# Two sparse-graph hops on one core: sources multiplied ahead of a branch, rows fetched earlier, own links added later

## The chip, the cores and the metric

The kernel runs on one core of one Trainium2 chip. The metric is the device time of one execution in microseconds; smaller is better. The engines are named as in the profile: PE (TensorE, with its weight loads as PEld), DVE (VectorE), ACT (ScalarE), POOL (GpSimd) and SP (SyncE, which here issues most of the DMAs). Each runs its own list of instructions in order, and they meet through semaphores.

## The reference, cut to what matters

Layer 0 is a graph attention over 4096 nodes, layer 1 a two-step diffusion. The part that the change touches is the second: in each step the features `Xf` are multiplied by the normalised 0/1 matrix `R` (the adjacency plus the unit matrix), and `Xa` by an attention matrix that keeps the top 90% of its probability.

```python
    R = S + jnp.eye(N, dtype=X.dtype)
    R = R / R.sum(-1, keepdims=True)
    Z = jnp.zeros_like(X)
    Xf = X
    Xa = X
    for n in range(STEPS):                     # STEPS = 2
        A = _top_p_attention(Xa, W1, W2, W3)
        Xf = R @ Xf
        Xa = A @ Xa
        Z = Z + Xf @ U1[n].T + Xa @ U2[n].T
    h = X + Z
    ...                                        # layer norm of h, and the sum with x
```

`X` is 4096 x 256 in float32, `S` the 4096 x 4096 adjacency.

## The kernel before, in words

Nodes are cut into NB = 32 blocks of 128 rows. Layer 0 comes first and leaves the adjacency in `adj_d`, arranged as 4 passes (`PASSES`) x 32 source blocks: the block `adj_d[p, :, j, :]` is 128 sources by 1024 targets, 512 KB. Then, for each step `n` of layer 1, there are two stages.

**A hop** (`R @ Xf`, lines 450 to 539). For each of the 128 pairs `(p, j)` in `order`, one edge block `ar` (every fifth one in a spare buffer, `aru`) and one row block of the source are needed. In hop 1 (step 0) the rows lie in SBUF as `X`. In hop 2 (step 1) they are read from `xf_d`, 128 KB each, into tiles named `x1` (three buffers) or `xa` (two). `fetched` (line 450) issues the two loads on SP, the edge block first. `split` (465) adds the unit matrix to the block where source and target coincide (line 468, on DVE; the "own link"), and cuts the source row into a high part (line 470, a cast on ACT) and the rest (line 471, on DVE), both in `hl`. `graph_products` (474) then multiplies: for each feature half `s` and term `t`, two matmuls, one for each 512 columns `c` of targets. The half `c = 0` is summed in the PSUM tile named `mm`, of which there are two with two banks each; the half `c = 1` in two tiles named `acc`. So there are 8 matmuls a source. `hops` (513) walks over the sources: in turn `n` it fetches source `n`, splits source `n - 1` and multiplies source `n - 5` (`LOOK = 4`); there are four `ar` buffers, one `aru`, and five of `hl`. It yields twice a source, and at each yield other work is put between the products: projections to keys and queries (`projections`, 592), tables of moments (lines 646 to 695, among them the copy of `mu` on line 660), the logits and exponentials of the first three attention blocks (`fills`, 1109; lines 578 and 738) and their search for a threshold (`picks`, 1129; lines 800, 824 and 831). At the end of a pass `drained` (480) copies the sums out.

**The attention** of the 32 blocks (lines 1209 to 1230). `attend` (941) transposes the exponentials in 8 groups (`turn`, line 911 on PE, copied to `eT` on ACT), multiplies them with `X` (`gather`, line 919), and runs the functions that the dictionary `between` has for a group. `contributed` (936) and `finish` (1081) apply the weights and add up.

In this code the order on each engine is written out by hand: within `tc.manual_schedule` an engine issues its instructions in the order in which the Python text makes them.

**The branch.** Between the steps stands `repaired` (1074): if any row's threshold was not found, some blocks are computed again, with `prepared` (1021) and `completed` (1050). In the run shown nothing is computed again; every engine jumps over that code (line 1075). Past the jump each engine waits until its own earlier work is done and then raises its semaphores by what the code jumped over would have raised them. What comes after the branch and uses a tile that this code uses too (an `mm` or `acc` tile in PSUM, an `xa` tile) waits for those raised semaphores of the other engines. A first jump of the same kind, line 1206, lies in the last attention block of a step.

In before, hop 2's first three sources are fetched just ahead of the last contributions of step 0 (line 1226, `early`). Their splits stand ahead of line 1075 on ACT and DVE, their products behind it on PE.

Of the kernel before, what the change touches and what calls it, by code (L numbers as in the profile page):

```python
# [26 lines left out]
P = 128  # L27
# [13 lines left out]
G0 = 8  # L41
# [15 lines left out]
def gat_then_top_p_diffusion(  # L57
# [108 lines left out]
    with tc.tile_pool(name="l0", bufs=1) as l0, tc.tile_pool(name="l0s", bufs=2) as l0s, tc.tile_pool(name="l0o", bufs=1) as l0o:  # L166
# [280 lines left out]
        PASSES = NB // G0  # L447
        S = SimpleNamespace(spare=None)

        def fetched(hop, n, p, j):  # L450

            r = SimpleNamespace(j=j, p=p)
            if S.spare is not None and n % 5 == 4:
                r.ar = S.spare.tile([P, G0 * P], F32R, name="aru", tag="u")
            else:
                r.ar = rp.tile([P, G0 * P], F32R, name="ar", bufs=4)
            nc.sync.dma_start(r.ar.bitcast(F32), adj_d[p, :, j, :].bitcast(F32))
            if hop == 0:
                r.src = X[:, j, :]
            else:  # L460
                r.src = S.rows.tile([P, D], F32, name="x1", bufs=3) if n % 5 < 3 else S.rows.tile([P, D], F32, name="xa")
                nc.sync.dma_start(r.src, xf_d[j])
            return r

        def split(r):
            if r.j // G0 == r.p:
                own = r.ar[:, ts(r.j % G0, P)]
                nc.vector.tensor_tensor(own, own.bitcast(F32), ident, ALU.add)
            hl = rp.tile([P, 2, D], F32R, name="hl", bufs=5)
            nc.scalar.copy(hl[:, 0, :], r.src)  # L470
            nc.vector.tensor_tensor(hl[:, 1, :], r.src, hl[:, 0, :].bitcast(F32), ALU.subtract)
            return r.ar, hl

        def graph_products(j, s, acc, ar, hl):
            for t in range(2):
                for c in range(2):
                    nc.tensor.matmul(acc[c][s], hl[:, t, ts(s, P)], ar[:, ts(c, 512)],  # L477
                                     start=(j == 0 and t == 0), stop=(j == NB - 1 and t == 1))

        def drained(hop, p, acc):  # L480
# [30 lines left out]
        order = [(p, j) for p in range(PASSES) for j in range(NB)]  # L511

        def hops(hop, early=()):

            fetch, ready, turned = dict(enumerate(early)), {}, []
            parted = 0
            for n in range(len(order) + LOOK + 1):
                if len(early) <= n < len(order):
                    fetch[n] = fetched(hop, n, *order[n])
                m = n - LOOK - 1  # L520
                held = m // NB * NB + NB + 2 if m >= 0 and m % NB > NB - 4 else len(order)
                while parted < min(n, len(order), held):
                    ready[parted] = split(fetch.pop(parted))
                    parted += 1
                if m >= 0:
                    p, j = order[m]
                    if j == 0:
                        wide = ps2.tile([P, 2, 512], F32, name="mm")
                        acc = [[wide[:, s, :] for s in range(KC)],
                               [ps1.tile([P, 2, D], F32, name="acc").rearrange("p t d -> p (t d)") for s in range(KC)]]  # L530
                    graph_products(j, 0, acc, *ready[m])
                    if turned and j > 2 and j % 2:
                        turned.pop(0)()
                    yield
                    graph_products(j, 1, acc, *ready.pop(m))
                    if j == NB - 1:
                        turned = drained(hop, p, acc)
                    yield
            S.turned = turned

        first_hop = hops(0)
# [46 lines left out]
    def waits(n):  # L588
        for i in range(n):
            yield  # L590

    def projections(cur, n, G):
# [59 lines left out]
        for g in range(NB // 8):  # L652
            pg = ps2.tile([P, 2, 512], F32, name="mm")
            for i in range(8):
                nc.tensor.matmul(pg[:, i // 4, ts(i % 4, DA + 1)], qT[:, ts(8 * g + i, P)].bitcast(F32), moments, start=True, stop=True)
# [4 lines left out]
            nc.scalar.copy(mu[:, ts(g, 8)].rearrange("p (h i) -> p h i", h=2), of[:, :, :, 0])  # L660
# [31 lines left out]
        nc.vector.tensor_scalar(far, far, -1.0, 1.0, ALU.mult, ALU.add)  # L692
        nc.vector.tensor_scalar(sg, sg, 1.0 / 0.64, None, ALU.mult)
        G.kT, G.qT, G.sg = kT, qT, sg
        yield from waits(6)

    def table(name):
        return small.tile([P, NB], F32, name=name, bufs=1)
# [322 lines left out]
    def prepared(R):  # L1021

        act, dve = index(R, ET.Activation), index(R, ET.DVE)
        q = rows.tile([2 * DA, P], F32R, name="a_q", tag="q_s", bufs=3)
        shift = col("a_nm", 1)
        nc.scalar.copy(q, R.qT[:, ds(act * P, P)].bitcast(F32))
        q = (q, swapped(q))
        nc.scalar.copy(shift, R.nm[:, ds(act, 1)])
        nc.vector.tensor_copy(R.t, R.table[:, ds(dve, 1)])
        sums = small.tile([P, 2, 4], F32, name="sums", bufs=6)  # L1030
        ev = R.e.rearrange("p (h c n) -> p h c n", h=2, c=4)

        def exponentials_again():
            for c in range(4):
                nc.scalar.activation(ev[:, :, c, :], logits(q, R.kT, c), AF.Exp, bias=shift, accum_out=sums[:, c // 2, c % 2:c % 2 + 1])
            nc.vector.tensor_tensor(sums[:, 0, :2], sums[:, 0, :2], sums[:, 1, :2], ALU.add)
            nc.vector.tensor_tensor(R.z, sums[:, 0, 0:1], sums[:, 0, 1:2], ALU.add)

        exponentials_again()
        with tc.If(number(R, R.failed) > 0):  # L1040

            m = small.tile([P, N // 1024], F32, name="m4", bufs=1)
            for c in range(N // 1024):
                nc.vector.tensor_reduce(m[:, c:c + 1], logits(q, R.kT, c), AX.XY, ALU.max)
# [105 lines left out]
    for n in range(STEPS):  # L1150
# [2 lines left out]
        found = [table(f"found{i}") for i in range(3)]  # L1153
        blocks = {}
        with tc.manual_schedule(engines=every):
            pieces = first_hop if n == 0 else hops(n, early)
            filling, picking = fills(n, G, found, blocks), picks(n, found, blocks)
            done = 0 if n else NB - G0 - LOOK
            for i, _ in enumerate(pieces, 2 * done):
# [104 lines left out]
```

## Time and profile before

| what | us |
|---|---|
| median of 3 runs | 2985.69 (2983.98 to 2989.06) |
| the profiled execution | 2990.15 |
| its span, first to last instruction | 2988.2 |
| PE busy / PEld busy | 2844.6 / 2477.4 |
| DVE busy / ACT busy / POOL busy | 2199.6 / 1918.9 / 725.7 |
| hop 1, first to last start of its products | 839.6 to 1152.3 |
| hop 2, first to last start of its products | 1905.2 to 2238.0 |
| median landing of an edge block `ar` / a row from `xf_d` into `x1` | 4.7 / 4.9 |

The page gives each engine's busy time, then the span in 40 equal slices with a digit for the busy tenths of each, the DMA queues, the chain of work that ended last, and groups of instructions with the idle time before them and what ended most of it ("<-"). Other views of the same trace list the instructions in order of time, all instructions of one source line, who waited for whom, and the busy time in chosen stretches. A line such as `PE mm L615 <- ACT xs L610: 2.6, 4, 1.4` says that PE, before line 615, waited for ACT's line 610 for 2.6 us in total, 4 times, the longest 1.4 us. "PEldq", "DVEq" and so on are an engine's sequencer: waiting, branching or issuing.

### The profile page before, as it was taken

Reading aid. Unit: us, or ns where it says so; the run is one execution under the profiler, and the core shown is the slowest. Engines: PE = TensorE matmul, PEld = TensorE weight load, DVE = VectorE, ACT = ScalarE, POOL = GpSimd, SP = SyncE. Lnnn points to the kernel's source line nnn. Section 1 sums busy time; section 2 is a strip of 40 time slices with the busy share of each in tenths; the row PEclk is TensorE's granted clock in tenths of the full one; section 3 lists DMA queues with packets and bytes.
Section 4 is the critical chain, followed back from the end, with each engine's and each line's share of the span. In section 5 each row is a group of like instructions: output and inputs, shape, how many; then the busy total and the mean of one; then the engine's idle time right before and its main releaser. Section 6 shows DMA issues by size and latency. Waiting matters only on the chain. (4 is left out here: it accounts for less than half of the span.)

```text
span 2988.2 us, 51984 instructions
## 1 busy us (share of the span) xinstructions
PE 2844.6 (95%) x19033; PEld 2477.4 (83%) x19033; DVE 2199.6 (74%) x5187; ACT 1918.9 (64%) x3075; POOL 725.7 (24%) x1637
## 2 busy tenths in 40 slices
PE   4699999999999999999999999798899999999998
PEld 3499999999977778888888888676678888888887
DVE  6666877868754383888888889242755999999996
ACT  5767687867823735777777775234427777777772
POOL 3201101111010210233222331000203444444442
PEclk7799999999999999999999999999999999999999
DMA  6859668695455784000000000577991001000000
GB/s 153 176 208 238 193 217 190 232 226 189 179 169 163 245 298 144 19 26 19 19 19 19 26 19 19 172 240 218 307 320 30 25 27 30 25 25 25 31 25 21
DMA packets 181151, 368.15 MB, mean 123 GB/s; under 512 B 17168, under 2 KB 133904, under 8 KB 176784
## 3 DMA queue, kind: packets, MB, share of 16 engines
q1 hardware_dynamic: 129824, 261.55, 26.8%
q0 software_dynamic: 21504, 83.89, 11.8%
q10 hardware_dynamic: 29552, 19.22, 2.1%
q8 instruction: 155, 2.54, 0.4%
q14 instruction: 116, 0.95, 0.1%
HBM read 301.35 MB, written 109.38 MB: 137 GB/s over the span
## 5 line engine op out<-in xcount | busy, mean ns | idle before, releaser
L919 PE MATMUL acc<-X,eT 128*128 128x256 f32 x4096 | 965.8, 381 | 0.0
L919 PEld LDWEIGHTS acc<-X,eT 128*128 128x128 f32 x4096 | 743.2, 190 | 97.4 <-ACT eT L913 14.6
L325 PE MATMUL acc<-ut,m 128*128 128x195 bf16 (+1 forms) x8192 | 701.2, 247 | 13.6 <-DVE m L305 8.0
L325 PEld LDWEIGHTS <-m 128*128 128x128 fp8e4 x8192 | 696.9, 97 | 17.9 <-issue 9.6
L738 ACT ACTIVATE e<-mm,nm 128x1024 f32<-128x1024 f32 x256 | 286.9, 1121 | 301.8 <-PE mm L578 288.4
L299 ACT ACTIVATE g<-sr,d_big 128x1024 uint8<-128x1024 f32 x448 | 471.3, 1140 | 5.4 <-DMA s_d<-sT 2.9
L477 PE MATMUL mm<-ar,hl 128*128 128x512 f32 x844 | 342.8, 406 | 25.7 <-DVEq L1075 10.9
L806 DVE SCALAR_TENSOR_TENSOR big<-e,c 128x4096 f32<-128x4096 f32 x58 | 273.0, 4708 | 121.3 <-POOL c L791 84.1
L913 ACT COPY eT<-tp 128x512 f32<-128x512 f32 x512 | 299.3, 585 | 95.6 <-PE tp L911 94.6
L824 DVE MAX8 cand<-big 128x8 f32<-128x228 f32 (+1 forms) x1152 | 348.3, 380 | 0.0
L762 POOL TENSOR_TENSOR sums<-sums 128x2 f32<-128x2 f32 x64 | 12.7, 198 | 1343.3 <-ACT void L745 1343.3
L477 PE MATMUL acc<-ar,hl 128*128 128x512 f32 x844 | 334.2, 396 | 0.6 <-ACT stage L488 0.6
L911 PE MATMUL tp<-ident,e 128*128 128x128 f32 x2048 | 310.6, 274 | 2.7 <-PEq L1206 0.6
L911 PEld LDWEIGHTS tp<-ident,e 128*128 128x128 f32 x2048 | 248.6, 141 | 71.8 <-ACT eT L933 27.8
L305 DVE TENSOR_TENSOR m<-g,ax 128x512 uint32<-128x512 uint32 x256 | 181.5, 709 | 127.3 <-PE acc L325 104.0
L848 DVE SCALAR_TENSOR_TENSOR e<-e,found 128x4096 f32<-128x4096 f32 x58 | 259.6, 4477 | 0.0
L745 ACT ACTIVATE void<-e,c1x 128x2048 int8<-128x2048 f32 x128 | 257.4, 2011 | 3.3 <-issue 2.9
L745 ACT ACTIVATE void<-e,c 128x2048 int8<-128x2048 f32 x128 | 257.4, 2011 | 2.0 <-issue 2.0
L477 PEld LDWEIGHTS mm<-ar,hl 128*128 128x128 f32 x844 | 161.5, 191 | 68.4 <-issue 13.5
L578 PE MATMUL mm<-kT,qT 128*128 128x512 f32 x512 | 199.2, 470 | 11.4 <-ACT e L738 10.4
L306 DVE TENSOR_TENSOR m<-m,ax 128x512 uint32<-128x512 uint32 x256 | 177.1, 692 | 25.3
L477 PEld LDWEIGHTS acc<-ar,hl 128*128 128x128 f32 x844 | 161.6, 191 | 32.7 <-ACT stage L488 1.0
(262 smaller groups left out, 3457.6 us busy)
## 6 DMA issues: line engine op xcount, KB each, us to landing
ar<-adj_d SPq DMA_DIRECT2D x211, 512.0 KB, 4.7
adj_d<-ax POOLq DMA_DIRECT2D x32, 2048.0 KB, 7.0
ut<-uv_d SPq DMA_DIRECT2D x60, 784.0 KB, 5.4
aru<-adj_d SPq DMA_DIRECT2D x45, 512.0 KB, 4.8
ax<-in_adj_t_dram POOLq DMA_DIRECT2D x32, 512.0 KB, 15.8
x<-xf_d SPq DMA_DIRECT2D x78, 128.0 KB, 4.9
uv_d<-st ACTq DMA_DIRECT2D x32, 294.0 KB, 4.2
xf<-xft_d SPq DMA_DIRECT2D x64, 128.0 KB, 2.3
```

The source lines that it names most:

```text
L299: nc.scalar.activation(g[:, c, :], shared[k].sr, AF.Relu, scale=BIG, bias=d_big[:, h, j:j + 1])
L325: nc.tensor.matmul(shared[k].acc[i][:, t, :cols], m[t][:, c, ts(i, P)], shared[k].ut[j // QUARTER][:, j % QUARTER, t, :cols], start=(j == ...
L477: nc.tensor.matmul(acc[c][s], hl[:, t, ts(s, P)], ar[:, ts(c, 512)], start=(j == 0 and t == 0), stop=(j == NB - 1 and t == 1))
L578: nc.tensor.matmul(pm[:, h, :], q[t], kT[:, ds(h * (N // 2) + c * 512, 512)], start=(t == 0), stop=(t == 1))
L738: nc.scalar.activation(ev[:, :, c, :], r.pm[c], AF.Exp, bias=r.nm, accum_out=r.sums[:, c // 2, c % 2:c % 2 + 1])
L745: nc.scalar.activation(void, r.e[:, ts(h, N // 2)], (AF.Relu, AF.Sign)[i], bias=r.c1, scale=-1.0, accum_out=r.sums[:, h, 2 + i:3 + i])
L806: nc.vector.scalar_tensor_tensor(big, r.e, r.c3, r.e, ALU.is_le, ALU.mult, accum_out=r.low3)
L824: nc.vector.max(cand[:, s, :], big[:, edges[s]:edges[s + 1]])
L848: nc.vector.scalar_tensor_tensor(r.e, r.e, r.t, r.e, ALU.is_ge, ALU.mult, accum_out=kept)
L911: nc.tensor.transpose(pt[:, i, :], r.e[:, ts(4 * g + i, P)], ident)
L913: nc.scalar.copy(eT, pt)
L919: nc.tensor.matmul(r.acc[:, 0, :], eT[:, i, :], cur[:, j, :], start=(j == 0), stop=(j == NB - 1))
```

## The change

- `fetched` becomes two functions, `source` (the row) and `edge` (the block). In turn `n` the row of source `n + 2` is fetched, and then the edge block of source `n`.
- `split` only cuts rows. The own link is added by `own`, which in turn `n` goes up to source `n - 3`; its product comes two turns later.
- `begin(second, 4)`, put at group 2 of the last attention block of step 0, issues the rows and edges of hop 2's first four sources. Their splits follow at groups 5 and 6, their own links at group 6.
- After that block's `contributed`, PE multiplies these four sources with the half `c = 0` of the targets: 16 matmuls, before the branch. After the branch the first four sources have only the half `c = 1` left (16 matmuls). The `mm` tile of the first half is held across the branch.
- In `prepared`, which lies inside the branch, products go through single PSUM banks named `tp` instead of `mm`: 8 pieces of 512 columns in place of 4 of 1024.
- The copy of `mu` moves from ACT to DVE, and the tables are followed by 10 yields instead of 6.

```diff
+        def source(A, n):
+            if n in A.src or n >= len(order):
+                return
+            if A.hop == 0:
+                A.src[n] = X[:, order[n][1], :]
+            else:
+                A.src[n] = S.rows.tile([P, D], F32, name="x1", bufs=3) if n % 5 < 3 else S.rows.tile([P, D], F32, name="xa")
+                nc.sync.dma_start(A.src[n], xf_d[order[n][1]])
+
+        def edge(A, n):
+            if n in A.ar or n >= len(order):
+                return
+            p, j = order[n]
             if S.spare is not None and n % 5 == 4:
-                r.ar = S.spare.tile([P, G0 * P], F32R, name="aru", tag="u")
+                ar = S.spare.tile([P, G0 * P], F32R, name="aru", tag="u")
             else:
-                r.ar = rp.tile([P, G0 * P], F32R, name="ar", bufs=4)
-            nc.sync.dma_start(r.ar.bitcast(F32), adj_d[p, :, j, :].bitcast(F32))
-            if hop == 0:
-                r.src = X[:, j, :]
-            else:
-                r.src = S.rows.tile([P, D], F32, name="x1", bufs=3) if n % 5 < 3 else S.rows.tile([P, D], F32, name="xa")
-                nc.sync.dma_start(r.src, xf_d[j])
-            return r
-
-        def split(r):
-            if r.j // G0 == r.p:
-                own = r.ar[:, ts(r.j % G0, P)]
-                nc.vector.tensor_tensor(own, own.bitcast(F32), ident, ALU.add)
-            hl = rp.tile([P, 2, D], F32R, name="hl", bufs=5)
-            nc.scalar.copy(hl[:, 0, :], r.src)
-            nc.vector.tensor_tensor(hl[:, 1, :], r.src, hl[:, 0, :].bitcast(F32), ALU.subtract)
-            return r.ar, hl
+                ar = rp.tile([P, G0 * P], F32R, name="ar", bufs=4)
+            nc.sync.dma_start(ar.bitcast(F32), adj_d[p, :, j, :].bitcast(F32))
+            A.ar[n] = ar
+
+        def split(A, n):
+            while A.parted < min(n, len(order)):
+                src = A.src[A.parted]
+                hl = rp.tile([P, 2, D], F32R, name="hl", bufs=5)
+                nc.scalar.copy(hl[:, 0, :], src)
+                nc.vector.tensor_tensor(hl[:, 1, :], src, hl[:, 0, :].bitcast(F32), ALU.subtract)
+                A.hl[A.parted] = hl
+                A.parted += 1
+
+        def own(A, n):
+            while A.owned < min(n, len(order)):
+                p, j = order[A.owned]
+                if j // G0 == p:
+                    block_ = A.ar[A.owned][:, ts(j % G0, P)]
+                    nc.vector.tensor_tensor(block_, block_.bitcast(F32), ident, ALU.add)
+                A.owned += 1
+
+        def graph_products(A, m, s, halves=(0, 1)):
+            j = order[m][1]
+            if j == 0 and s == 0:
+                if 0 in halves:
+                    wide = ps2.tile([P, 2, 512], F32, name="mm")
+                    A.acc = [[wide[:, s, :] for s in range(KC)], None]
+                if 1 in halves:
+                    A.acc[1] = [ps1.tile([P, 2, D], F32, name="acc").rearrange("p t d -> p (t d)") for s in range(KC)]
             for t in range(2):
-                for c in range(2):
-                    nc.tensor.matmul(acc[c][s], hl[:, t, ts(s, P)], ar[:, ts(c, 512)],
+                for c in halves:
+                    nc.tensor.matmul(A.acc[c][s], A.hl[m][:, t, ts(s, P)], A.ar[m][:, ts(c, 512)],
                                      start=(j == 0 and t == 0), stop=(j == NB - 1 and t == 1))
...
+        def begin(A, n):
+            for i in range(n):
+                source(A, i)
+                edge(A, i)
+            A.begun = n
+
+        def hops(A):
+
+            turned = []
+            for n in range(A.begun, len(order) + LOOK + 1):
+                for i in range(3 if n == A.begun else 1):
+                    source(A, n + 2 - (2 - i if n == A.begun else 0))
+                edge(A, n)
                 m = n - LOOK - 1
-                held = m // NB * NB + NB + 2 if m >= 0 and m % NB > NB - 4 else len(order)
-                while parted < min(n, len(order), held):
-                    ready[parted] = split(fetch.pop(parted))
-                    parted += 1
+                split(A, min(n, m // NB * NB + NB + 2) if m >= 0 and m % NB > NB - 4 else n)
+                own(A, m + 3)
                 if m >= 0:
                     p, j = order[m]
...
+                    halves = (1,) if m < A.begun else (0, 1)
+                    graph_products(A, m, 0, halves)
...
-            nc.scalar.copy(mu[:, ts(g, 8)].rearrange("p (h i) -> p h i", h=2), of[:, :, :, 0])
+            nc.vector.tensor_copy(mu[:, ts(g, 8)].rearrange("p (h i) -> p h i", h=2), of[:, :, :, 0])
...
-        yield from waits(6)
+        yield from waits(10)
...
+        def columns(c):
+            pm = ps2.tile([P, 4, P], F32, name="tp").rearrange("p a b -> p (a b)")
+            for t in range(2):
+                nc.tensor.matmul(pm, q[t], R.kT[:, ts(c, 512)], start=(t == 0), stop=(t == 1))
+            return pm
...
-            attend(r, cur, blocks[NB - 2], None, {0: beginning, 3: earlier})
+            beside = {0: beginning, 3: earlier}
             if n + 1 < STEPS:
-                early = [fetched(n + 1, i, *order[i]) for i in range(3)]
+                second = hop_of(n + 1)
+                beside.update({2: lambda: begin(second, 4), 5: lambda: split(second, 2), 6: lambda: (split(second, 4), own(second, 4))})
+            attend(r, cur, blocks[NB - 2], None, beside)
             contributed(r, contribute(r))
+            for m in range(second.begun if n + 1 < STEPS else 0):
+                for s in range(KC):
+                    graph_products(second, m, s, (0,))
             finish(r)
```

More of the change, by code (lines that the diff above doesn't have):

```diff
@@ L448, in gat_then_top_p_diffusion, with hop_of @@
         S = SimpleNamespace(spare=None)
-        def fetched(hop, n, p, j):
-            r = SimpleNamespace(j=j, p=p)
+        order = [(p, j) for p in range(PASSES) for j in range(NB)]
+        def hop_of(hop):
+            return SimpleNamespace(hop=hop, src={}, ar={}, hl={}, acc=None, begun=0, parted=0, owned=0)
+        def source(A, n):
[6 more added lines that the diff above has]
+                nc.sync.dma_start(A.src[n], xf_d[order[n][1]])
@@ L463, in fetched @@
-            return r
-        def split(r):
-            if r.j // G0 == r.p:
-                own = r.ar[:, ts(r.j % G0, P)]
-                nc.vector.tensor_tensor(own, own.bitcast(F32), ident, ALU.add)
-            hl = rp.tile([P, 2, D], F32R, name="hl", bufs=5)
-            nc.scalar.copy(hl[:, 0, :], r.src)
-            nc.vector.tensor_tensor(hl[:, 1, :], r.src, hl[:, 0, :].bitcast(F32), ALU.subtract)
-            return r.ar, hl
-        def graph_products(j, s, acc, ar, hl):
+                ar = rp.tile([P, G0 * P], F32R, name="ar", bufs=4)
@@ L509, in drained @@
             return [stored] + ([lambda c=c, i=i: by_rows(c, i) for c in range(2) for i in (0, 2)] if hop + 1 < STEPS else [])
[L511 to L519, printed above, removed]
+        def begin(A, n):
[9 more added lines that the diff above has]
+                edge(A, n)
                 m = n - LOOK - 1
-                held = m // NB * NB + NB + 2 if m >= 0 and m % NB > NB - 4 else len(order)
-                while parted < min(n, len(order), held):
-                    ready[parted] = split(fetch.pop(parted))
-                    parted += 1
+                split(A, min(n, m // NB * NB + NB + 2) if m >= 0 and m % NB > NB - 4 else n)
+                own(A, m + 3)
                 if m >= 0:
                     p, j = order[m]
[L527 to L531, printed above, removed]
+                    halves = (1,) if m < A.begun else (0, 1)
+                    graph_products(A, m, 0, halves)
                     if turned and j > 2 and j % 2:
@@ L534, in hops @@
                     yield
-                    graph_products(j, 1, acc, *ready.pop(m))
+                    graph_products(A, m, 1, halves)
                     if j == NB - 1:
-                        turned = drained(hop, p, acc)
+                        turned = drained(A.hop, p, A.acc)
                     yield
             S.turned = turned
-        first_hop = hops(0)
+        first_hop = hops(hop_of(0))
         with tc.manual_schedule(engines=every | {ET.SP}):
@@ L1029, in prepared @@
         nc.vector.tensor_copy(R.t, R.table[:, ds(dve, 1)])
-        sums = small.tile([P, 2, 4], F32, name="sums", bufs=6)
-        ev = R.e.rearrange("p (h c n) -> p h c n", h=2, c=4)
+        sums = small.tile([P, N // 512], F32, name="a_sums", bufs=1)
+        def columns(c):
[3 more added lines that the diff above has]
+            return pm
         def exponentials_again():
[L1034 to L1037, printed above, removed]
+            for c in range(N // 512):
+                nc.scalar.activation(R.e[:, ts(c, 512)], columns(c), AF.Exp, bias=shift, accum_out=sums[:, c:c + 1])
+            nc.vector.reduce_sum(R.z, sums, axis=AX.X)
         exponentials_again()
         with tc.If(number(R, R.failed) > 0):
-            m = small.tile([P, N // 1024], F32, name="m4", bufs=1)
-            for c in range(N // 1024):
-                nc.vector.tensor_reduce(m[:, c:c + 1], logits(q, R.kT, c), AX.XY, ALU.max)
+            m = small.tile([P, N // 512], F32, name="a_max", bufs=1)
+            for c in range(N // 512):
+                nc.vector.tensor_reduce(m[:, c:c + 1], columns(c), AX.X, ALU.max)
             nc.vector.tensor_reduce(shift, m, AX.X, ALU.max, negate=True)
@@ L1155, in gat_then_top_p_diffusion @@
         with tc.manual_schedule(engines=every):
-            pieces = first_hop if n == 0 else hops(n, early)
+            pieces = first_hop if n == 0 else hops(second)
             filling, picking = fills(n, G, found, blocks), picks(n, found, blocks)
```

## The prediction

> **What bounds the kernel now.** I read the page's 40 slices first, to see where TensorE (PE) is not full.
>
> ```profile
> PE   4699999999999999999999999798899999999998
> PEclk7799999999999999999999999999999999999999
> DMA  6859668695455784000000000577991001000000
> GB/s 153 176 208 238 193 217 190 232 226 189 179 169 163 245 298 144 19 26 19 19 19 19 26 19 19 172 240 218 307 320 30 25 27 30 25 25 25 31 25 21
> ```
>
> A slice is 74.7 us. PE is full except at the start and in slices 25 to 29, about 1890 to 2240 us: the branch after step 0 and hop 2. The change touches that stretch, and hop 1 (slices 11 to 15), where PE is full. Next, PE's timeline across the branch, and the rows of line 1075, the branch itself.
>
> ```profile
> 1893.28 1.03 PE L939 MATMUL acc<-u,eT 128*128 128x256 f32 x4
> 1905.23 0.77 PE L477 MATMUL mm<-ar,hl 128*128 128x512 f32 x1 [10.93 <-DVEq L1075]
> 1905.80 0.63 PE L477 MATMUL acc<-ar,hl 128*128 128x512 f32 x1
> ...
> 1915.35 0.39 PE L477 MATMUL mm<-aru,hl 128*128 128x512 f32 x1
> ```
>
> ```profile
> L1075 DVEq EVENT_SEMAPHORE  x2: 21/21/21, 1905.0 to 1905.1; - x2
> L1075 PEldq COMPARE_BRANCH  x1: 5152/5152/5152, 1893.1 to 1893.1; - x1
> ...
> L1075 DVEq COMPARE_BRANCH  x1: 67/67/67, 1901.9 to 1901.9; - x1
> ```
>
> PE's own branch takes 5.15 us, to 1898.3. It then waits for VectorE (DVE), whose branch is issued only at 1901.9, after the third of hop 2's splits, and whose semaphore past it comes 3.1 us later, at 1905.0. PE idles 10.93 us. Its next 14 matmuls start 0.43 us apart and the later ones 0.23. Source 4 (the first `aru`) starts at 1915.35.
>
> Then the waits inside hop 2: those of ScalarE (ACT) on line 470, and PE's waits in 1990 to 2080.
>
> ```profile
>   DMA x<-xf_d: 89.6, 49
>   DMA xa<-xf_d: 71.3, 39
>   DVE ar L468: 20.3, 11
> ```
>
> ```profile
> PE mm L578 <- ACT e L738: 5.5, 3, 4.8
> PE mm L655 <- ACT mu L660: 3.5, 1, 3.5
> ```
>
> ```profile
> 2049.06 0.40 ACT L470 CAST hl<-x 128x256 fp32r<-128x256 f32 x1 [1.24 <-DMA x<-xf_d]
> 2050.64 0.40 ACT L470 CAST hl<-xa 128x256 fp32r<-128x256 f32 x1 [1.17 <-DMA xa<-xf_d]
> 2050.95 1.11 ACT L738 ACTIVATE e<-mm,nm 128x1024 f32<-128x1024 f32 x1
> ```
>
> ACT stands 160.9 us in hop 2 waiting for rows; what is queued behind the casts waits with it. The timeline shows the exponential starting straight after two casts that each waited for a row; PE has waited 4.83 us for it when it resumes at 2052.20. Last, the stretches of hop 2:
>
> ```profile
> 2020.00:2060.00 40.00, 32.02 (x136) 26.23 (x137) 14.37 (x42) 8.79 (x24) 0.00 (x0) 0.83 0.62 188
> 2140.00:2180.00 40.00, 37.73 (x159) 29.11 (x159) 34.95 (x99) 9.11 (x22) 0.00 (x0) 1.00 0.95 328
> 2180.00:2220.00 40.00, 36.65 (x154) 27.83 (x153) 19.92 (x59) 7.22 (x18) 0.00 (x0) 1.00 0.98 332
> ```
>
> The columns are PE, weight load, DVE, ACT and POOL busy, PE's clock, DMA share, GB/s. Early in hop 2 the DMA engines have room (0.62), late they do not (0.98 at 332 GB/s).
>
> [...]
>
> **The change, part by part.**
>
> *Ahead of the branch.* Four edge blocks and four rows are now issued on SP in the last block of step 0. SP is past its inner branch at 1877.1 and its next issue, the store of `xa`, is at 1892.11; eight issues of 0.43 to 0.51 take 3.8 us. They move ahead of that store and of z's, and delay neither. In 1860 to 1871 the DMA share is 0.03, so landing takes 4.7 us (edges) or 5.0 (rows) and all is there before 1887. Four casts on ACT (0.41 each, two at a time) fit its 1.58 us gaps between `eT` copies; DVE's four subtractions (0.43) and four own links (0.29) lie in its 18.73 us idle stretch. Cost on PE's path: nothing; with this cover gone it would be a cast pair, 0.8 us, twice.
>
> Behind the last contribution come 16 matmuls (4 sources, 2 feature halves, 2 terms, one of the two column halves) at full clock: 16 x 0.227 = 3.6 us. DVE now reaches its branch right after line 1086 (ends 1895.28), so it is past it at about 1898.1. SP no longer has loads outstanding there, only z's store. The last to pass becomes PE itself: its branch is issued 3.6 us later, 1896.8, and ends 5.15 later at 1901.9; with semaphores, work begins at about 1902.2, 3.0 earlier. The gap is still some 4.3 us, so I price the restart at half clock: 14 x 0.43 + 2 x 0.23 = 6.5 us for the other 16 half products, to 1908.7. SP's load of source 4 waits for PE's release past the branch, so it goes at 1902.3 and edge 4 at about 1903.7; it landed and had its link 4.0 us after issue before, so 1907.8: in time. Source 4 then starts at 1908.7 instead of 1915.35: 6.6 us won. The load of X for the first projection (issue to landing 5.4) is reached sooner by PE than it lands: 0.3 back. **Gain 6.3.** Bounds: PE's other passage of this branch took 3.87 instead of 5.15, 1.3 more gained; if PE's restart waited for something else until 1905, the products ahead alone give 3.6 less the wait of source 4, about 3.
>
> *Rows two ahead.* Each row is issued two sources, some 3.7 us, sooner, the issue count unchanged. ACT's row waits average 160.9 / 88 = 1.8 us, the longest 6.4, so most vanish. What PE gets of it, stage by stage from its idle gaps over 0.2 us:
> - 1920 to 2010, projections: 1.44 + 0.34 + 1.04 + 0.61 + 0.21 + 0.95 + 0.30 = 4.9, behind `xs`, `kT` and `qT`, partly these engines' own chains. I take half, **2.5**.
> - 2010 to 2060: 3.50 before line 655, and about 1.0 of half-clock matmuls after it; 4.83 + 0.21 before line 578, and 12 matmuls 0.2 us slower after it, 2.4. Together 12.0. Both have ACT and DVE stuck in splits that wait for rows. The move of the `mu` copy (0.17 each, x4 per hop) to DVE takes away the second cross-engine wait. I take **10.5**.
> - 2060 to 2110: 0.48 + 2.40 + 1.38 = 4.3, all before line 578, with ACT in casts that wait for rows. **3.0**.
> - 2110 to 2210: gaps of 9.5, before products waiting for line 470 or 471, with DMA at 0.92 to 0.98. A row that comes sooner makes its edge block come later at the same bandwidth: 640 KB per source at 332 GB/s is 1.97 us, the products take 1.85. Also DVE's chain of `best` (4.2 us without a split) remains. **2.5**, bounds -3 and 6.
>
> *Own links late.* In before, a link that waits for its edge block holds the split behind it (26.9 us of such waits on DVE in hop 1, 19.9 in hop 2). Now it stands after the split, two turns ahead of its product. Hop 1 needs no row loads; its PE gaps before products at 863, 1054 and 1081 us lie behind DVE's normalisation and `best` chain, which stay. **1.0** for hop 1, bounds -1 and 3; hop 2's is within the numbers above.
>
> *No cost:* four more yields before the first exponentials (the picking of three blocks ends well before the hop does; PE has products meanwhile); the redo by single banks (no instruction of line 1035 ran), which only frees the wide bank to be held across the branch. If it ran, it would be longer.
>
> Sum: 6.3 + 2.5 + 10.5 + 3.0 + 2.5 + 1.0 = 25.8. The profiled execution took 2990.15 (span 2988.2 and 1.95 around it), so 2964.4 by its own time; the median shown, 2985.69, is 4.5 lower, and 2959.9 is my figure, 2960.
>
> A cross-check: from its ninth source to its last, hop 1 takes 299.8 us and hop 2 310.8; PE's gaps in these stretches are 14.2 us in the first, 9.4 of them after 880, and 26.3 with 3.4 of half clock in the second. Hop 2 with hop 1's 9.4 would take 20.3 less; my parts for it sum to 18.5.
>
> **Rivals.**
> 1. *DMA takes the place of the rows* (chance 0.22). Freed of row waits, PE asks 640 KB in 1.85 us; edge blocks come late instead. For it: the 0.98 share, landings of up to 8.4 us. Against: 0.62 to 0.81 where most of the gain lies. Then the branch and half the middle remain: 6.3 + 5 + 1 = 12, 2974.
> 2. *Everything goes* (0.12): all gaps of hop 2, and the restart at full clock: 6.3 + 2.8 + 4.9 + 12.0 + 4.3 + 6 = 36, 2950. Against: own chains of DVE and ACT seen in hop 1.
> 3. *Slower: SP stands before edges* (0.06). A row's load now precedes the edge on SP, and waits until the split three sources back has freed its buffer. Where DVE lags three sources (5.6 us), no edge is issued. In the picking of three blocks there are three `best` chains of 4.2 us and twelve half passes of 2.35, together 41 us in which it could. Against a gain of 25.8 it decides once 63% of them stall PE; at 85% they cost 35, and the time is 2960 + 35 = 2995. Against: splits finish early once rows do.
> The forecast itself has 0.60.
>
> **Numbers.** Range 2947 to 2976: it takes in rivals 1 and most of 2. About 0.2%, 6 us, is what a measurement here tells from no change. Slower by more 0.06, within 0.03, faster 0.91.
>
> **What would show it.** PE's gap at the branch about 4 us, released by PE's own branch; source 4 some 6 us sooner after step 0's last product; ACT's waits for `x` and `xa` from `xf_d` under 40 us; no gap over 1.5 before lines 655 and 578; DMA share over 0.8 early in hop 2. Wrong: a gap still ending with DVE, waits of PE for `ar`, or SP's line of the row load waiting for DVE for tens of us.

## The result and the profile after

The changed kernel takes 2958.76 us, the median of 6 runs (2953.83 to 2960.24), beside 2984.48 for the kernel before (6 runs, 2980.75 to 2989.06). The ratio is 0.9911, with a 95% interval of 0.9899 to 0.9924: 25.7 us less. 2960 us were forecast.

To see where the time came from I cut both profiled executions at the same events: products of hop 1, the last contribution of step 0 (PE's matmul on line 963, before 939), and the first product of certain sources of hop 2. The table's figures are differences of start times in the two traces.

| stretch | before | after | difference |
|---|---|---|---|
| hop 1, first to last product | 312.6 | 316.1 | +3.5 |
| step 0's attention, to its last contribution | 741.7 | 745.6 | +3.9 |
| from there to source 4 | 21.4 | 9.8 | -11.6 |
| source 4 to source 8 | 13.6 | 14.7 | +1.1 |
| source 8 to 32 (projections) | 77.8 | 71.2 | -6.6 |
| source 32 to 48 | 57.8 | 43.7 | -14.1 |
| source 48 to 64 | 40.9 | 35.9 | -5.0 |
| source 64 to 96 | 67.5 | 65.0 | -2.5 |
| source 96 to the last product | 64.9 | 63.1 | -1.8 |
| step 1's attention | 750.2 | 754.1 | +3.9 |
| span | 2988.2 | 2958.3 | -29.9 |

Hop 2 gave 40.6 us (its seven rows, each rounded, add to 40.5). Both attention stages, in which the forecast saw nothing to gain or lose, took 3.9 back each. The page's slices, now 74.0 us each, show the first of these:

```profile
PE   4699999999999999999999999899999999999998
PEclk8799999999999999999999999999999999999999
DMA  6858668595454686000000000388980000001000
```

The 7 and the two 8s that PE showed from the branch to the end of hop 2 have become one 8, in the slice of the branch; DMA is busy in five slices there instead of six; the granted clock, as before, is a 9 from the third slice on.

PE's timeline across the branch follows (start, duration, the matmuls; in brackets the idle time before them and what ended it), and then the rows of line 1103, which is the branch (duration min/median/max in ns, then the first and last start).

```profile
1900.80 3.77 PE L502 MATMUL mm<-ar,hl 128*128 128x512 f32 x15
...
1904.87 0.47 PE L502 MATMUL mm<-ar,hl 128*128 128x512 f32 x1 [0.30 <-PEq L1103]
...
1905.17 3.83 PE L502 MATMUL acc<-ar,hl 128*128 128x512 f32 x16
...
1910.59 0.47 PE L502 MATMUL mm<-aru,hl 128*128 128x512 f32 x1 [1.58 <-DMA aru<-adj_d]
```

```profile
L1103 DVEq EVENT_SEMAPHORE  x2: 21/21/21, 1904.6 to 1904.7; - x2
...
L1103 PEldq COMPARE_BRANCH  x1: 3732/3732/3732, 1900.5 to 1900.5; - x1
L1103 DVEq COMPARE_BRANCH  x1: 67/67/67, 1901.7 to 1901.7; - x1
```

The gap of 10.93 us is 0.30. PE's sequencer reached its branch at 1900.5, before the first of the 16 products ahead had even started (1900.80). Fifteen of them were queued already, and PE worked on them while its sequencer jumped for 3.73 us; the sixteenth starts past it, at 1904.87. Why it did not run with the others is open. DVE jumped in the same time, 1901.7 to 1904.6. Behind this short gap the 16 of the other half start 0.23 us apart, and the granted clock is 1.00 (1905.10 to 1909.00); in before, behind the 10.93 us, it was 0.50 (1905.20 to 1911.00), with starts 0.43 us apart. Full and half clock stand for these two here and in the forecast. What comes next is a new wait: PE reaches source 4 before its edge block has landed (1.58 us). SP issued that block only at 1906.90, behind the rows of sources 4 to 6.

ACT's and PE's waits in hop 2, 1900 to 2206 (total us, times, the longest), of the changed kernel:

```profile
ACT hl L479 <- PE acc L502: 39.6, 24, 3.2
ACT hl L479 <- DMA x<-xf_d: 36.2, 22, 3.0
ACT hl L479 <- DMA xa<-xf_d: 32.2, 17, 7.3
```

```profile
PE mm L502 <- DMA aru<-adj_d: 4.0, 2, 2.4
PE tp L633 <- DMA X<-xa_d: 3.3, 1, 3.3
PE mm L502 <- ACT hl L479: 2.0, 1, 2.0
PE mm L502 <- DMA ar<-adj_d: 1.9, 4, 0.8
PE mm L602 <- ACT e L762: 1.1, 3, 0.4
```

ACT's waits for rows fell from 160.9 to 68.4 us, and its largest single group is now a wait for PE's products: ACT is as far ahead as the five `hl` tiles let it be. On PE the moments' wait for `mu` (3.5) is no longer listed, and the 4.83 us before the logits are 0.4 at most. What PE waits for most is now a DMA. The stretches (columns as before) show that the DMA engines have become full late in hop 2 (a share of 0.99 at 348 GB/s, where before had 0.95 at 328):

```profile
2020.00:2060.00 40.00, 38.87 (x167) 30.83 (x166) 11.78 (x39) 22.96 (x43) 0.00 (x0) 1.00 0.82 265
...
2140.00:2180.00 40.00, 37.58 (x158) 30.26 (x157) 24.83 (x75) 9.38 (x23) 0.00 (x0) 0.96 0.99 348
```

Where the 3.9 us twice went shows in the other branch, that of the last attention block (line 1234, before 1206). PE's timeline there, and the rows of its line:

```profile
1877.35 1.89 PE L943 MATMUL acc<-X,eT 128*128 128x256 f32 x8
1881.82 0.63 PE L935 MATMUL tp<-ident,e 128*128 128x128 f32 x4 [2.58 <-DVEq L1234]
1882.28 3.35 PE L943 MATMUL acc<-X,eT 128*128 128x256 f32 x8
```

```profile
L1234 DVEq EVENT_SEMAPHORE  x4: 21/21/21, 1881.7 to 2931.0; - x4
...
L1234 PEldq COMPARE_BRANCH  x2: 231/300/369, 1876.4 to 2924.8; - x2
L1234 DVEq COMPARE_BRANCH  x2: 68/70/72, 1878.7 to 2928.0; - x2
```

PE's own jump is short here, 0.23 and 0.37 us. But its next transposes write a `tp` tile, and the redo behind this branch now uses `tp` tiles. So PE waits until DVE has passed too, 3.0 us after DVE's branch. The gap is 2.58 us in step 0's attention and 3.18 in step 1's, 0.30 in before, and the eight gathers after it take 3.35 us instead of 1.89: most of them start 0.43 us apart instead of 0.22, which is half clock (granted 0.55 in 1882.20 to 1885.50, against 1.00 in 1877.30 to 1879.20, ahead of the gap).

### The profile page after: what moved, and what is told of

It is laid out like the page before. It is cut to its first block, busy times and chain, and to the rows that moved or that the text cites. A ratio compares the mean times of both kernels' runs of the same rounds, so it can differ in the third digit from the quotient of the medians.

```text
span 2958.3 us, 51979 instructions
## 1 busy us (share of the span) xinstructions
PE 2829.7 (96%) x19033; PEld 2473.5 (84%) x19033; DVE 2196.5 (74%) x5195; ACT 1915.5 (65%) x3067; POOL 726.4 (25%) x1637
## 5 line engine op out<-in xcount | busy, mean ns | idle before, releaser
L502 PE MATMUL mm<-ar,hl 128*128 128x512 f32 x844 | 336.6, 402 | 13.1 <-DMA ar<-adj_d 5.4
L935 PEld LDWEIGHTS tp<-ident,e 128*128 128x128 f32 x2048 | 249.3, 141 | 77.2 <-ACT eT L957 27.8
## 6 DMA issues: line engine op xcount, KB each, us to landing
ax<-in_adj_t_dram POOLq DMA_DIRECT2D x32, 512.0 KB, 15.7
```

Source lines behind the costliest of these rows:

```text
L502: nc.tensor.matmul(A.acc[c][s], A.hl[m][:, t, ts(s, P)], A.ar[m][:, ts(c, 512)], start=(j == 0 and t == 0), stop=(j == NB - 1 and t == 1))
L935: nc.tensor.transpose(pt[:, i, :], r.e[:, ts(4 * g + i, P)], ident)
```

## The experiments

Theory A, after the comparison: the gain is the branch (some 10 us) and rows fetched ahead (the rest of hop 2); the redo by single banks costs 7.8 us, though none of it runs; own links and `mu` matter little. The rivals are named with each run. In all these kernels the whole computation is done. Each was measured beside the kernel before in the same job, where that took 2984.67 us (first four runs), 2993.78 (next four) and 2985.79 (last three); stretches are from the profiled executions.

**The redo takes the `mm` bank again at the inner branch only** (from the changed kernel).

```diff
-    def prepared(R):
+    def prepared(R, wide=False):
-            pm = ps2.tile([P, 4, P], F32, name="tp")...
+            pm = bank() if wide else ps2.tile([P, 4, P], F32, name="tp")...
-                    prepared(R)
+                    prepared(R, wide=True)
```

> The changed kernel, with the redo inside the inner branch of the last attention block going through an mm tile again (the redo behind the outer branch stays in tp). Nothing is left out. Theory (the tp tiles make PE's next transposes wait until DVE has passed the inner branch, 2.58 us and some matmuls at half clock, once a step): both gaps go back to about 0.3 us, each step ends 3.9 us sooner, 7.8 us below the changed kernel, about 2951. Rival (the gap comes from DVE's place in the last block, whichever bank the redo uses): no change, 2959.

2951.02 us, ratio 0.988 (0.9857 to 0.9902). The attention stages are 741.7 and 750.0 again, hop 2 304.4. PE's timeline at the inner branch of this kernel:

```profile
1877.02 1.89 PE L943 MATMUL acc<-X,eT 128*128 128x256 f32 x8
1879.21 0.63 PE L935 MATMUL tp<-ident,e 128*128 128x128 f32 x4 [0.30 <-PEq L1234]
1879.67 1.89 PE L943 MATMUL acc<-X,eT 128*128 128x256 f32 x8
```

The gap and the half clock are gone. So code that is jumped over cost the changed kernel 7.7 us by the tiles that it names, and that is shown by this one edit: in the traces the attention stages give back 3.9 and 4.1. In step 1 the price depends on a second part of the change, as the run with links before splits shows.

**Rows fetched in the turn of their edge** (from the changed kernel; links stay late).

```diff
-                for i in range(3 if n == A.begun else 1):
-                    source(A, n + 2 - (2 - i if n == A.begun else 0))
                 edge(A, n)
+                source(A, n)
```

> The changed kernel, with each row fetched in the turn of its edge block again, behind it. Theory of the prediction (row waits on ACT are what PE lost early and in the middle of hop 2): ACT's waits for rows of xf_d come back to about 150 us, gaps of PE before the logits and the moments come back, 15 to 20 us slower than the changed kernel, about 2976. Rival (own links ahead of the split, and mu on ACT, held DVE and ACT; the rows' place matters little): under 6 us slower, 2964 or less.

3009.64 us, ratio 1.0082 (1.0061 to 1.0102): slower than before, which neither theory had. Hop 2 took 357.1 us. A wait of PE's in this kernel's hop 2, and then those of ACT:

```profile
PE acc L502 <- DVE aru L489: 7.1, 3, 4.9
```

```profile
ACT hl L479 <- DMA x<-xf_d: 96.9, 51, 5.2
ACT hl L479 <- DMA xa<-xf_d: 87.8, 41, 9.1
```

Rows are late again (184.7 us of waits), and now DVE's link of an earlier source stands behind a split that waits for its row; PE waits for that link (line 489), which it did not in the changed kernel. The two edits are not a sum: late links are harmless only with early rows. That called for the four combinations below.

**Own links before their splits** (from the changed kernel; rows stay two ahead).

```diff
-                split(A, min(n, m // NB * NB + NB + 2) if m >= 0 and m % NB > NB - 4 else n)
-                own(A, m + 3)
+                held = min(n, m // NB * NB + NB + 2) if m >= 0 and m % NB > NB - 4 else n
+                for k in range(A.parted, min(held, len(order))):
+                    own(A, k + 1)
+                    split(A, k + 1)
```

> The changed kernel, with each own link added just ahead of its source's split again, both in the same turn. Theory (late links cost hop 1 about 4 us, where PE waits for a link that stands behind a half pass on DVE, and gain in hop 2 what DVE no longer waits for edge blocks): hop 1 4 us shorter, hop 2 2 to 5 us longer, in sum within 3 us of the changed kernel. Rival (late links are a large part of hop 2's gain): hop 2 10 us or more longer.

2959.06 us, ratio 0.9908 (0.9887 to 0.9929), the changed kernel's time. Hop 2 is 4.4 us longer in the profile (307.8), but DVE's passage at the inner branch of step 1, from its branch to its next semaphore, took 0.6 us instead of 2.8, which gave 3.7 back. The rows of that branch, to be read beside those of line 1234 above:

```profile
L1236 DVEq EVENT_SEMAPHORE  x4: 21/21/21, 1880.0 to 2931.3; - x4
...
L1236 DVEq COMPARE_BRANCH  x2: 68/70/72, 1877.0 to 2930.6; - x2
```

The short passage goes with the links' place. It stands in the traces of all five kernels that add links ahead of splits (before, before with `tp`, this one, and the two below that have rows in their edge's turn and links before splits) and in none of the eight that add them after, where it is 2.8 to 3.1. So late links are worth at most 4.4 us in hop 2, and with the redo in `tp` they cost 3.7 at the inner branch in this pair of traces. Hop 1 took 314.7, against 316.1 with late links and 313.7 in the kernel with `mm` banks above, whose hop 1 is the changed kernel's code: links make no difference there that stands out from the repeats.

**No products ahead of the branch** (from the changed kernel; sources are still fetched and split ahead).

```diff
-                    halves = (1,) if m < A.begun else (0, 1)
+                    halves = (0, 1)
-            for m in range(second.begun if n + 1 < STEPS else 0):
-                for s in range(KC):
-                    graph_products(second, m, s, (0,))
```

> The changed kernel without products ahead of the branch: rows, edges, splits and links of the first four sources stay there, all their 32 matmuls come behind it. Theory (PE's branch is issued while the 16 matmuls are still queued, so they cover its 3.7 us): the gap at the branch goes from 0.3 to about 4 us, and the restart is at half clock for some 14 matmuls (2.8 us), about 6.5 us slower, 2965. Rival (DVE's earlier branch alone brought the gain, the products ahead only change places): under 3 us slower.

2956.63 us, ratio 0.9904 (0.9885 to 0.9923): no loss. Its timeline at the branch, and the rows of the branch:

```profile
1897.54 1.03 PE L963 MATMUL acc<-u,eT 128*128 128x256 f32 x4
1902.06 0.80 PE L502 MATMUL acc<-ar,hl 128*128 128x512 f32 x1 [3.48 <-DVEq L1103]
1902.65 0.63 PE L502 MATMUL mm<-ar,hl 128*128 128x512 f32 x1
1903.08 0.63 PE L502 MATMUL acc<-ar,hl 128*128 128x512 f32 x1
```

```profile
L1103 DVEq EVENT_SEMAPHORE  x2: 21/21/21, 1902.0 to 1902.1; - x2
...
L1103 PEldq COMPARE_BRANCH  x1: 3555/3555/3555, 1897.4 to 1897.4; - x1
L1103 DVEq COMPARE_BRANCH  x1: 67/67/67, 1899.1 to 1899.1; - x1
```

(One of the 32 products still ran ahead of the branch here, at 1895.49.) The gap and the half clock (0.43 us between most of the starts) are back, yet source 8 comes only 3.3 us later after the last contribution (27.8 against 24.5), and at the end of hop 2 1.7 are left of that. Before the change source 8 came after 35.0. So of the 10.5 us won at the branch some 7 belong to the splits and fetches that were moved ahead of it: DVE's branch is now issued 1.6 us after that contribution starts (1897.54 to 1899.1), where it was 8.6, behind three splits (1893.28 to 1901.9). The products themselves are worth 3.3 at most, and the times show nothing of it: this kernel's median lies 2.1 us under that of the changed one. With them PE waits longer for X (3.3 us against 1.9) and for edge blocks.

**Only the work ahead of the branch** (the changed kernel with rows in their edge's turn, links before splits, `mu` on ACT, and six yields; edits as shown).

> Of the change only what is put ahead of the branch (loads, splits, links and half products of four sources) and the redo in tp; rows in their edge's turn, links ahead of the split, mu on ACT and 6 yields as in before. The branch's part by itself. Theory: 10.5 us gained to source 8, 7.8 lost at the two inner branches, so 2 to 4 us below before, about 2982. Rival (what is gained at the branch is given back further on in hop 2, where DMA is the limit): 5 us above before or more.

2984.38 us (20 runs), ratio 0.9974 (0.9964 to 0.9983). Hop 2 335.3, 8.8 less than before; 3.9 of it goes back at the first inner branch. The ratio rests on the 2993.78 of this job; beside the 2984.5 to 2985.8 of the others there is no gain, so the times leave open whether this part pays alone.

**The same with `mu` on DVE and ten yields.**

> The kernel with only rows ahead undone and with links ahead of the split again: against own_before it shows rows two ahead alone, against rows_late it shows what late links do while rows are late. Theory (a late link stands behind a split that waits for its row, so late links cost much while rows are late, and rows ahead are worth about 16 us by themselves): 2975, hop 2 about 322, some 35 us shorter than with late rows and late links. Rival (rows ahead are worth the 50 us that taking them back alone cost): about 3005.

2988.34 us (9 runs), ratio 0.9985 (0.9972 to 0.9997); hop 2 334.8, so `mu` and the yields did nothing there that shows. Against the run with links before splits (307.8) only the rows differ: **fetching two ahead is worth 27.0 us of hop 2**. The medians of the two, from different jobs, lie 29.3 apart, and 23 by their ratios. Against the run with late rows (357.1) only the links differ: late links with late rows cost 22.3. What the 27.0 consist of shows in the projections' matmuls and their weight loads (PEld), 1900 to 2240, in this kernel and then in the one with rows two ahead (busy us, mean ns of one, idle time before):

```profile
L640 PE MATMUL mm<-wkq,xs 128*128 128x128 f32 x128 | 18.5, 288 | 2.7 <-ACT xs L635 2.4
...
L640 PEld LDWEIGHTS mm<-wkq,xs 128*128 128x128 f32 x128 | 15.5, 191 | 7.7 <-ACT xs L635 7.7
```

```profile
L641 PE MATMUL mm<-wkq,xs 128*128 128x128 f32 x128 | 15.6, 275 | 0.0
L641 PEld LDWEIGHTS mm<-wkq,xs 128*128 128x128 f32 x128 | 15.5, 192 | 0.6
```

The same 128 matmuls not only wait less, they are also busy 2.9 us less. This is not half clock: their loads average 191 and 192 ns in the two kernels. With late rows the loads wait 7.7 us for `xs`, in place of 0.6, and the matmuls' line shows 2.7 of that as idle; the rest passes while an earlier matmul still counts as busy. The 64 matmuls of the moments (line 680, then 681) are busy 1.7 us less, 7.7 instead of 9.4, and wait for `mu` 1.2 instead of 4.6. Here it is half clock: after the wait some loads take 0.33 us instead of 0.19, and their mean is 226 ns against 192.

Summed over hop 2, PE's idle time falls by 16.2 us (31.9 to 15.7), and the other 10.8 are matmuls that start closer together. By the distances of their starts some 4.4 of these are half clock (35 loads over 0.3 us in this kernel, 6 in the other) and 3.0 the waits of the projections' loads; the last 3.4 are small delays that I did not trace.

**Only `mu` on ACT and six yields** (from the changed kernel).

```diff
-            nc.vector.tensor_copy(mu[...], of[:, :, :, 0])
+            nc.scalar.copy(mu[...], of[:, :, :, 0])
-        yield from waits(10)
+        yield from waits(6)
```

> The changed kernel with the copy of mu on ACT and 6 yields again. Theory (with rows in time, ACT is not late for mu): under 4 us slower, 2963 or less. Rival (mu on ACT and the exponentials' earlier place were a large part of the 14 us won between sources 32 and 48): 2966 or more, with a gap of 3 us before the moments' matmuls.

2958.5 us, ratio 0.988 (0.9863 to 0.9897), hop 2 305.2 against 303.4: no effect that shows. In before, ACT's copy of `mu` (line 660) had waited 19.2 us in all, 7 times, for DVE's `sq` (line 658). With late rows the gap before the moments was there with either engine, 3.10 us with ACT and 3.65 with DVE.

**The wait for source 4's edge block, tried away** (from the kernel with `mm` banks): edge block 4 is issued ahead of rows 5 and 6, and the first fills of step 1 come two sources later.

```diff
+                source(A, n)
+                if n == A.begun:
+                    edge(A, n)
+                    source(A, n + 1)
+                source(A, n + 2)
                 edge(A, n)
-                if (n == 0 or i > 10) and i // 2 % NB != NB - 2:
+                if (n == 0 or i > 14) and i // 2 % NB != NB - 2:
```

> The kernel with the redo of the inner branch in mm; besides, behind the branch the edge block of source 4 is issued before the rows of sources 5 and 6, and in step 1 the first projection starts four yields later. Theory (PE's 1.6 us wait for that block and 3.3 us for the first X vanish, the rest stays): 3 to 5 us below the kernel with the redo in mm, about 2947. Rival (DMA is the limit behind the branch, the wait only moves): 2951.

2950.95 us, ratio 0.9858 (0.9841 to 0.9875). Source 8 comes after 19.3 us instead of 25.0, but 4.7 of these 5.7 lie behind source 4, where the first fills no longer stand. Ahead of source 4 PE still waits, 1.1 us for the block and 1.3 for its link. Sources 48 to 64 take 40.6 instead of 35.9, and the span is 2949.4 against 2950.8: the fills that were put off take their time later.

**The kernel before, with the redo in `tp` tiles** (the two loops of `prepared` as in the change, nothing else).

> The kernel before, with nothing changed but the redo, which goes through single tp banks in both branches. Nothing is left out. Theory (the redo's bank alone costs a wait for DVE at the inner branch of each step): 7.8 us slower than before, a gap of about 2.6 us before the transposes behind each inner branch in place of 0.3. Rival (the cost comes only with the loads that the change puts behind that branch): no change.

2987.76 us (20 runs), ratio 1.0006 (0.9998 to 1.0014): not the 7.8 us expected. PE's gaps:

```profile
1877.75 0.63 PE L911 MATMUL tp<-ident,e 128*128 128x128 f32 x4 [2.58 <-DVEq L1210]
...
1898.08 0.51 PE L477 MATMUL mm<-ar,hl 128*128 128x512 f32 x1 [2.69 <-ACT hl L470]
1906.44 0.80 PE L477 MATMUL acc<-ar,hl 128*128 128x512 f32 x1 [7.85 <-DVEq L1079]
```

The wait at the inner branch came as expected in step 0's attention, but no half clock followed it (2.1 us in all). In step 1's DVE's passage took 0.6 us, as it does where links come before splits, so that the cost there was 0.2. The trace thus has 2.3 us of cost in place of 7.8, and the medians differ by 2.0. Hop 2 took 5.2 less. Since the redo no longer uses `mm` tiles, one product went ahead of the outer branch, but that split the gap of 10.93 and hardly shortened it: source 8 came 0.9 sooner. The other 4.3 lie behind source 8, where the two kernels are the same, so that a difference of this size in hop 2 can come from one execution to the next.

**Rows one turn ahead** (from the changed kernel).

```diff
-                for i in range(3 if n == A.begun else 1):
-                    source(A, n + 2 - (2 - i if n == A.begun else 0))
+                for i in range(2 if n == A.begun else 1):
+                    source(A, n + 1 - (1 - i if n == A.begun else 0))
```

> The changed kernel with rows fetched one source ahead of their edge block, not two. Theory (ACT's waits for rows averaged 1.8 us, and a source takes 1.85, so one turn takes most of them away): within 8 us of the changed kernel, 2967 or less. Rival (a row takes 5 us to land, and one turn more than none still leaves ACT waiting): 12 us slower or more, 2971 and up.

2960.54 us, ratio 0.9918 (0.9901 to 0.9934), hop 2 306.5: one turn brings nearly all.

**Links one turn earlier** (from the kernel with `mm` banks).

```diff
-                own(A, m + 3)
+                own(A, m + 4)
```

> The kernel with the redo of the inner branch in mm, and own links added three turns ahead of their product in place of two. Theory (PE's waits for a late link behind DVE's long instructions vanish, 1.4 and 2.9 us in hop 1): 2 to 4 us below the kernel with the redo in mm. Rival (hop 1's length varies by as much from run to run with unchanged code, and DVE now waits for edge blocks instead): the same within 2 us.

2946.81 us, ratio 0.9871 (0.9854 to 0.9887), against 0.988 without it: the intervals overlap, and hop 1 took 314.3 against 313.7. These three kernels with `mm` banks at the inner branch beat the changed kernel by 8 to 12 us; among themselves they can't be told apart.

## Why the prediction was right, and where it was not

The median is 1.2 us below the forecast. That it is so close is luck, since errors of opposite sign lie in the sum: in the traces some 16 us more were won in hop 2 than its terms give, and some 11 that no term has were lost in the attention and in hop 1.

*Ahead of the branch*: 6.3 forecast; 10.5 measured to source 8 in the changed kernel, 9.9 where it stands alone. The step that failed is "The last to pass becomes PE itself: its branch is issued 3.6 us later, 1896.8". In the changed kernel's trace PE's sequencer goes on to the branch while matmuls wait in PE's queue: the branch was issued 0.3 us before the first of the 16 started, and 15 ran beneath its 3.73 us. The lines that the prediction shows had it already: in before, PE's branch was issued at 1893.1, ahead of the contributions of line 939 at 1893.28. The gap of "some 4.3 us" and the restart at half clock, both priced on top, did not come (0.30 us, granted clock 1.00). That source 4 is "in time" failed too: PE started it 11.6 us sooner instead of 6.6, and that after 1.58 us of waiting for the block, which was issued at 1906.90 and not at 1903.7. From there to source 8 it lost 1.1 again, with a wait for X of 3.33 us where before had 1.0; 0.3 were forecast for that.

*Rows two ahead*: 18.5 forecast, 27.0 measured by the pair of runs that differ in nothing else. By its terms: projections 2.5 against 6.5, 2010 to 2060 10.5 against 11.4, 2060 to 2110 3.0 against 3.3, the next stretch 2.5 against 5.7 (sources 8 to 32, 32 to 48, 48 to 64, 64 to 96). The mechanism was right, and in the two middle stretches the size too. What was mis-sized is the projections' term, "I take half". Of PE's idle time there 2.4 us went (3.7 to 1.3), as much as the term has. The rest are waits that the idle time of matmuls does not show, 3.0 of them before the weight loads of the projections. The 5.7 lie inside the bounds of their term; the kernel with the work ahead alone took 68.6 in that stretch, not 71.8, so about 3 of them can be chance. In the 2010 to 2060 term, where I had counted half clock, the figure held, though the half clock was undercounted: the trace before has some 5.9 us of it there, by the distances of the starts, and not 3.4. ACT's waits were to fall under 40 us and fell to 68.4; with 7.3 us of that at the branch itself, the rest still cost PE 2.0 us in all, so that the sum of an engine's waits was a poor measure of what PE gets.

*Own links late*: 1.0 forecast for hop 1, none shown: hop 1 is 316.1, 313.7 and 313.7 in three kernels with the same hop 1, before's 312.6 lies beside them. In hop 2 they gave up to 4.4 in one pair of profiles, about what hop 2 varied by itself, and nothing in the times, where 3.7 went back at step 1's inner branch.

*"No cost"*: the ten yields and `mu`, right. The redo by single banks, wrong: "no instruction of line 1035 ran" was true and not the question. The description of the kernel states that what uses a tile of the jumped code waits for the other engines past the jump; I applied it to `mm` at the outer branch and not to `tp` at the inner one. It cost 7.7 us, half of it in step 1, where late links had to come to it.

In the cross-check the two lengths run from the eighth source on; from the ninth they are 298.0 and 309.0. The result does not rest on them.

The sum, from the profiles: hop 2 from the last contribution on took 344.1 before, 335.3 with the work ahead (8.8 gained), 334.8 with `mu` and the yields (0.5), 307.8 with the rows (27.0) and 303.4 with the late links (4.4): 40.7. Less 3.9 twice in the attention and 3.5 in this execution's hop 1 that is 29.4; the spans differ by 29.9, the medians by 25.7.

*The rivals.* DMA did become full late in hop 2 (0.97 to 0.99 at up to 348 GB/s) and PE's waits for edge blocks rose to 5.9 us, but that is small beside the gain: rival 1's mechanism without its price. No run tested that stretch alone, so how much DMA still holds back there is open. Rival 2, that all of hop 2's gaps go, came closest in hop 2 by its size (40.6 measured, 36 forecast), which the redo's cost hid. Its mechanism did not come about: PE still idles 14.3 us there, of 40.2 before. Rival 3's wait exists in the changed kernel:

```profile
SPq L462 <- DVE hl L480: 18.5, 22, 3.1
```

It is 22 short waits, not 41 us in the picking of blocks. More than the 5.9 us for which PE waited for edge blocks it cannot have cost through them. The loss that did exist with rows and links came the other way round, from late rows with late links (3009.64).

## What to carry to other kernels

Count what code behind a branch names, not what it runs: here a tile in jumped code tied the next user of that buffer to DVE's passage (3.0 us from its branch to its semaphore; PE's own jump took 0.23). Bring the other engines to their branch early, which was worth some 7 us here; matmuls queued ahead filled PE's jump (15 of them in its 3.73 us), but were worth 3.3 at most and nothing in the times. When pricing a gap of PE, look at the pace of the matmuls after it (14 stood 0.43 us apart in before, behind 10.93 us of idle time, though after gaps of 2.6 to 2.7 us not in every kernel), and at the waits of the weight loads, of which the idle time of the matmuls showed 2.7 of 7.7 us in the projections. Test coupled edits in all four combinations: early rows and late links were coupled, and so were late links and the redo in `tp`.

## What the runs showed of the hardware that was not expected

- DVE's passage past a jump, from its branch to its next semaphore, took 2.8 to 3.2 us, but 0.6 at the inner branch of step 1 in all five kernels that add own links before splits (before, before with `tp`, links before splits, and the two with only the work ahead), and in none of the eight others. With one trace of each kernel that is seen and not tested, but it points to the program and not to chance; why is open.
- PE's jump at the outer branch took 5.15 us after step 0 and 3.87 after step 1 in before, 3.73 and 3.56 in the changed kernel; at the inner one 0.23 and 0.38 in before, 0.23 and 0.37 in the changed kernel.
- A gap of 2.6 to 2.7 us at the same place, the inner branch of step 0, was followed by half clock in seven kernels (in the changed one eight gathers took 3.35 us) and not in two, before with `tp` (2.58 us, eight gathers in 1.89) and rows in the turn of their edge. In the kernel without products ahead a gap of 3.43 at step 1's inner branch was not followed by it either.
- Behind the outer branch of before a weight load took 0.33 us while the granted clock was 0.50 (1905.8 to 1910.9), and 0.19 where it was 1.00 (1911.25 to 1915.0); at the changed kernel's inner branch it took 0.34 and 0.19. In these traces that tells half clock from a load that waited.
- The same kernel before gave medians of 2984.5, 2984.7, 2985.8 and 2993.8 us in four jobs, while the changed kernel with `mu` moved back, measured beside the 2993.8, took 2958.5, as the changed kernel did elsewhere (2958.76). A ratio from that one job is some 0.3% lower for that.
